# Three buffers of sums instead of four, loaded one place sooner, and three store buffers for the x side and the early sums

## The chip, the cores and the metric

The kernel runs on one core of one Trainium2 chip. The metric is the device time of one execution in microseconds, as the median of the runs. PE is TensorE, PEld its weight loads, DVE is VectorE, ACT ScalarE, POOL GpSimd and SP SyncE; SP issues nearly all DMAs.

## The reference, cut to what matters

Four graph layers on x (64 graphs, 256 nodes, 256 features) with a residual and a layer norm after each. The change touches the first alone, which is a recurrence over the nodes:

```python
d = jnp.sum(adj, axis=-1)
norm_adjT = jnp.swapaxes(adj, 1, 2) * dinv[:, :, None]      # dinv = 1 / d, or 0
def step(h, i):
    x = jnp.take(h_e, i, axis=1)
    row = jnp.take(norm_adjT, i, axis=1)
    x_par = jnp.einsum('bj,bjd->bd', row, h)                # all nodes, the new ones before i
    iou = x @ W_ioux.T + b_ioux + x_par @ W_iouh.T + b_iouh
    r, z = jnp.split(iou, 2, axis=1)
    r, z = (jax.nn.sigmoid(r), jax.nn.sigmoid(z))
    hc = jnp.tanh(x @ W_coux.T + b_coux + x_par * r @ W_couh.T + b_couh)
    h_new = z * x_par + (1.0 - z) * hc
    return jax.lax.dynamic_update_slice(h, h_new[:, None, :], (0, i, 0)), None
h_out, _ = jax.lax.scan(step, h_e, jnp.arange(256))
x = layernorm(x + h_out)
```

## The kernel before, in words

The kernel has three stretches. A head makes, for the first half of the nodes, the part of `x_par` that comes from the old states x (nodes not yet updated), and stores it in a DRAM tensor `Us`. Then 256 steps of the recurrence run, one node each, for all 64 graphs at once. Then the layers 1 to 3 follow graph by graph; the change does not touch them.

**Steps, places, blocks.** Step n stands at place p = n % 8 in block a = n // 8; i = n % 32 is its place in a group of 32 nodes. The loop over the steps has a schedule by hand: each engine runs its instructions in the order in which the program writes them. At the end of each step stand the DMA issues of that step.

**Sums.** `sums[a]`, the tile `ACC` (128 x 8 x 128, 512 KB), holds the unfinished sums of `x_par` for the eight nodes of window a. `sums_in(a)` (line 313) allocates it and loads the x part from `Us` (L316). To it are added: the products with states just made, on DVE (`push`, L645) and on ACT and POOL (`scale_far`, L687, L692, L696; they reach as far as the next window); the `early` part, on POOL at places 3 and 4 (L853), made with states long before and kept in DRAM tensors `Es`; and the `late` part, on POOL at places 6 and 7 (L913). `ready` (L840) is the last reader of a row of `ACC`.

**Early part.** At place 0, `early_in_part(n + 16)` (L453) loads the early part of window a + 2; it is added to `sums[a + 2]` at places 3 and 4 of the same block. Windows from 8 on (node 64) have one, from 24 on (node 192) two.

**Late part.** At places 0 to 3 PE multiplies the states in the ring `Hw` with the adjacency (L531); `send` writes the result to DRAM (`Lb`, L511), `receive` loads it as `late_sb` (L517), and L913 adds it to the next window.

**Fills.** At places 4 to 7 PE has spare work in each step (`fill_early`): the early products (`early`, L424, from states `Hs` and adjacency `A`), or else the x side for the second half of the nodes (`x_side`, `xp`, L213). Their results go from PSUM into a tile `ub` (128 x 4 x 256) by copies on ACT (L256; in the trace `xu` and `eu`), and one step after the second copy, two DMAs store the tile to `Us` (L220) or `Es` (L436). Before, the pool gives `ub` two buffers, so the first copy into a new `ub` waits until the store of the tile two before has landed. The copies stand in a list (`copy_later`, `next_of`) and are taken at fixed points of a step; on ACT the copy at the end of a step stands ahead of the next step's copy `xpT` (L629), for which PE waits with its next matmuls (L620).

**Flush.** At i = 8 and i = 16 (both place 0) `flush` (L655) writes 15 or 16 states per half from the ring to DRAM, two DMAs of packets of 32 KB. The issues of a step's end stand on SP's list in this order: stores that fell due, the early part (place 0), the sums (place 1), xq (place 2), state and flush, the loads of the queue `loads` (state tiles `Hs`, adjacency `A`, `xA`, `xX`; L269).

Before, the sums have four buffers: windows 0, 1 and 2 are loaded ahead of the steps, window 3 in step 1, and at place 1 of block a window a + 3, into the buffer of window a - 1:

```python
            if p == 0 and n + 2 * U < N:
                early_in_part(n + 2 * U)
            if p == 1 and n + 3 * U < N:
                sums_in(n // U + 3)
```

Of the kernel before, what the change touches and what calls it, by code (L numbers as in the profile page):

```python
# [9 lines left out]
F32 = mybir.dt.float32  # L10
# [9 lines left out]
P = 128  # L20
# [50 lines left out]
def _recurrence(tc, ident, Hd, x, adj, W_ioux, b_ioux, W_iouh, b_iouh, W_coux, b_coux, W_couh, b_couh, wide, then):  # L71
# [20 lines left out]
    B, N, D = x.shape  # L92
    T = 32
    NB = N // T
    U = 8
# [8 lines left out]
    with ExitStack() as ctx:  # L104
# [21 lines left out]
        blk = ctx.enter_context(tc.tile_pool(name="r_blk", bufs=2))  # L126
# [83 lines left out]
        def x_product(pb, at, A, Xs):  # L210

            for jc, (a, xs) in enumerate(zip(A, Xs)):
                nc.tensor.matmul(  # L213
                    pb[:, at, :], a, xs, start=(jc == 0), stop=(jc == len(A) - 1)
                )

        def x_out(half, b, ub):

            for c in range(2):
                nc.sync.dma_start(  # L220
                    Us[c, b:b + 4, half * P:(half + 1) * P, :].rearrange("b i f -> i b f"),
                    ub[:, :, c * P:(c + 1) * P],
                )
# [30 lines left out]
        def copy_later(out, in_, then=None):  # L254
            def f(n):
                nc.scalar.copy(out, in_)  # L256
                held.pop(0)
                if then:
                    then(n)

            copies.append(f)

        def load_later(out, in_, rank):

            begun = []

            def f(n):
                with nc.allow_non_contiguous_dma(reason="bias vector across partitions"):
                    nc.sync.dma_start(out, in_)  # L269
                begun.append(n)  # L270

            loads.append((rank, f))
            loads.sort(key=lambda e: e[0])
            return begun

        def landed(begun, n):

            return all(f and n > f[0] + 2 for f in begun)

        def at_step(n, f):  # L280
            transfers.setdefault(n, []).append(f)
# [3 lines left out]
        def base_bank(shape, name):  # L285

            while len(held) == 3:
                next_of(copies, now)
            held.append(name)
            return ps.tile(shape, F32, tag="base", name=name, bufs=3)  # L290
# [21 lines left out]

        def sums_in(a):

            sums[a] = ACC = blk.tile([P, U, P], F32, tag="ACC", name=f"ACC_{a}", bufs=4)
            nc.sync.dma_start(  # L316
                ACC, Us[:, :, a * U:(a + 1) * U, :].rearrange("c b i f -> (c b) i f")
            )
# [3 lines left out]
        def x_side():  # L322

            def load(g):
                A = stream.tile([P, XB, P], F32, tag="xA", name=f"xA2_{g}", bufs=3)
                Xs = stream.tile([P, XB, D], F32, tag="xX", name=f"xX2_{g}", bufs=3)
                return A, Xs, [
                    load_later(to, of.rearrange("b j d -> j b d"), 2)
                    for to, of in ((A, adj[g:g + XB, P:N, P:N]), (Xs, x[g:g + XB, P:N, :]))
                ]  # L330

            def cut(A):
                nc.gpsimd.tensor_mul(A, A, tri.unsqueeze(1).to_broadcast([P, XB, P]))

            tiles = [load(e * XB) for e in range(3)]
            ahead = False
            n = yield
            for g in range(0, B, XB):
                A, Xs, last = tiles.pop(0)
                while not ahead:  # L340
                    if landed(last, n):
                        cut(A)
                        ahead = True
                    n = yield
                ahead = False
                ub = stream.tile([P, 4, D], F32, tag="ub", name=f"xu2_{g}")
                for b in range(0, XB, 2):
                    pb = base_bank([P, 2, D], f"xp2_{g}_{b}")
                    for q in range(2):
                        x_product(pb, q, [A[:, b + q, :]], [Xs[:, b + q, :]])  # L350
                        if q:
                            copy_later(ub[:, b:b + 2, :], pb, None if b + 2 < XB else (
                                lambda n, b=g, ub=ub: at_step(n + 1, lambda: x_out(1, b, ub))
                            ))
                            if b + 2 == XB and g + 3 * XB < B:
                                tiles.append(load(g + 3 * XB))
                        if not ahead and tiles and landed(tiles[0][2], n):

                            cut(tiles[0][0])
                            ahead = True  # L360
                        n = yield
# [13 lines left out]
        early_ub = []  # L375
# [36 lines left out]
        def early_fill(n):  # L412

            if early_pb:
                pb, e = early_pb.pop(), 1
            else:
                if not early_in or not landed(early_in[0][0], n):
                    return False
                _, k, lo, _, t = early_in[0][0:5]
                pb, e = base_bank([P, 2, D], f"early_{k}_{lo}_{t}"), 0  # L420
                early_pb.append(pb)
            _, k, lo, hi, t, Hs, A = early_in[0]
            for q in range(4):
                nc.tensor.matmul(  # L424
                    pb[q * T:(q + 1) * T, e, :], A[0:hi - lo, t % 2 * GB + e * 4 + q, :],
                    Hs[0:hi - lo, e * 4 + q, :], start=True, stop=True,
                )
            if e:
                early_in.pop(0)
                if t % 2 == 0:  # L430
                    early_ub[:] = [stream.tile([P, 4, D], F32, tag="ub", name=f"eu_{k}_{lo}_{t}")]
                ub = early_ub[0]

                def store():
                    for c in range(2):
                        nc.sync.dma_start(  # L436
                            Es[k, lo][c, 2 * t - 2:2 * t + 2].rearrange("n q i f -> (q i) n f"),
                            ub[:, :, c * P:(c + 1) * P],
                        )

                copy_later(
                    ub[:, t % 2 * 2:t % 2 * 2 + 2, :], pb,
                    (lambda n: at_step(n + 1, store)) if t % 2 else None,
                )
            return True

        def early_in_part(first):

            k, i = divmod(first, T)
            for (kk, lo), E in Es.items():  # L450
                if kk == k:
                    part = blk.tile([P, U, P], F32, tag="early", name=f"early_sb_{first}_{lo}")
                    nc.sync.dma_start(  # L453
                        part, E[:, :, :, i:i + U, :].rearrange("c n q i f -> (c n q) i f")
                    )
                    early_parts.append((first, part))
# [106 lines left out]
        def chain_S(k):  # L563

            Sd = blk.tile([P, T], F32, tag="Sd", name=f"Sd_{k}")
            flat = tables[k]["S"].rearrange("p j i -> p (j i)")
            first = (LAG - 1) * T
            nc.vector.tensor_mul(
                Sd, flat[:, first:first + (T - 1) * (T + 1) + 1:T + 1],
                dinv[:, k * T:(k + 1) * T],  # L570
            )
            return Sd
# [128 lines left out]
        sums = {}  # L701
# [9 lines left out]
        with tc.tile_pool(name="r_first_ps", bufs=4, space=bass.MemoryType.PSUM) as xps:  # L711
            for g in range(0, B, GB):
# [4 lines left out]
                for n in range(0, GB, 4):  # L717
                    ub = fst.tile([P, 4, D], F32, tag="ub", name=f"xu_{g}_{n}")
# [25 lines left out]
        stream = ctx.enter_context(tc.tile_pool(name="r_stream", bufs=2))  # L744
        work = ctx.enter_context(tc.tile_pool(name="r_work", bufs=2))
        ps = ctx.enter_context(tc.tile_pool(name="r_ps", bufs=1, space=bass.MemoryType.PSUM))

        sums_in(0)
        warm = work.tile([P, P], F32, tag="ready", name="warm", bufs=1)[:, 0:1]
        nc.vector.memset(warm, 0.0)  # L750
        nc.scalar.activation(warm, warm, AF.Sigmoid)
        tables[0]["An"] = late_load(0)
        tables[0]["Sd"] = chain_S(0)
        for a in range(1, 3):
            sums_in(a)
        for e in range(2):
            flip_x(0, e, xq[0])
            next_of(copies, 0)
# [26 lines left out]
        def fill_early(n):  # L785
            nonlocal x_left
            if not early_fill(n):
                for _ in range(2 if p in (6, 7) else 1):
                    if x_left and not fill(x_left, n):
                        x_left = None  # L790

        ctx.enter_context(tc.manual_schedule())
        for now in range(N):
            n = now
            k, i = divmod(n, T)
            p = n % U
# [119 lines left out]
            for f in transfers.pop(n, ()):  # L916
                f()
            if p == 0 and n + 2 * U < N:
                early_in_part(n + 2 * U)
            if p == 1 and n + 3 * U < N:  # L920
                sums_in(n // U + 3)
            if p == 2 and n // U + 2 < N // U:
                xq[n // U + 2] = load_x(n // U + 2)
            if i == U:
# [584 lines left out]
def kernel(ctx: ExitStack, tc: tile.TileContext, ins, out):  # L1509
# [14 lines left out]
    def load_layers(load):  # L1524
        weights.extend(
            _load_layers(nc, wide, load, ins["L1_gnn_W"], ins["L1_gnn_b"], l2, l3)
        )

    _recurrence(
        tc, ident, Hd, x, adj,  # L1530
        *(ins["L0_gnn_" + n] for n in (
# [44 lines left out]
```

## Time and profile before

| | |
|---|---|
| median of 3 runs | 3242.15 us (3241.41 to 3253.62) |
| profiled execution | 3241.76 us, span 3239.9 us |
| mean granted TensorE clock | 0.978 |
| PE busy in the span | 3038.5 us (94%) |
| DVE, ACT, POOL busy | 2611.5, 1949.4, 1882.3 us |
| head, steps, layers | 0 to 133, 133 to 1425, 1425 to 3240 us |

The span is that of the instructions on the core; the execution's time is 1.9 us longer. A step begins here where the copy `xpT` (L629) starts on ACT, so that step lengths are distances between such copies: 5.04 us in the mean, by place (medians) 6.08, 4.95, 4.69, 4.69, 4.63, 4.64, 4.64, 4.64. Landing times of loads are read from the DMA packets in the trace.

### The profile page before, as it was taken

The page shows a single profiled execution, that of the slowest core. Times are in us where ns is not written, and L with a number is a line of the kernel's source. Part 1 is how long each engine was busy: PE and PEld are TensorE (multiplying, and loading weights), DVE is VectorE, ACT ScalarE, POOL GpSimd, SP SyncE. Part 2 cuts the span into 40 slices and gives each one's busy share as a digit, 9 for nine tenths or more (in the row PEclk, how much of TensorE's full clock was granted, in tenths as well). Part 3 has the DMA queues.
Part 4 walks back from the last instruction along what each step waited for, and adds up shares of the span by engine and source line. Part 5 has one row for each costly group of instructions (what it writes and reads, how often), then busy time and mean ns, then how long its engine had stood idle before and what let it go on. Part 6 is the DMA issues. An engine that isn't in the chain of part 4 may idle for free.

```text
span 3239.9 us, 80388 instructions
## 1 busy us (share of the span) xinstructions
PE 3038.5 (94%) x28076; PEld 2257.2 (70%) x28076; DVE 2611.5 (81%) x7425; ACT 1949.4 (60%) x5160; POOL 1882.3 (58%) x2226
## 2 busy tenths in 40 slices
PE   4799999999999998958999999999999999999997
PEld 3566665655566665636888888888888888888885
DVE  2477776877678878745999999999999999999986
ACT  0166666666566666634666666666666666666664
POOL 2276777776677788733555555555555555555543
PEclk8899999999999999988999999999999999999998
DMA  9866777777776764434344444444444444444421
GB/s 304 255 165 144 195 175 177 175 174 190 182 185 151 193 159 133 100 71 92 81 89 88 88 87 88 88 89 88 88 88 88 88 89 89 89 89 89 89 50 30
DMA packets 954189, 402.54 MB, mean 124 GB/s; under 512 B 664524, under 2 KB 929880, under 8 KB 950104
## 3 DMA queue, kind: packets, MB, share of 16 engines
q1 hardware_dynamic: 935768, 379.42, 50.2%
q10 hardware_dynamic: 18016, 17.96, 1.8%
q8 instruction: 224, 3.67, 0.5%
q14 instruction: 181, 1.48, 0.2%
HBM read 278.53 MB, written 99.61 MB: 117 GB/s over the span
## 4 chain that ended last, share of the span: by engine, by line
PE 83%; DVE 6%; DMA 5%; issue 2%; SPq 1%; POOL 1%; ACT 1%; ACTq 0%; DVEq 0%; POOLq 0%
PE mm L1048 14%; PE rc L620 8%; PE rc L612 5%; PE late L531 4%; PE s L1279 4%; PE mm_2f L1048 4%; PE mm_3v L1048 4%; PE mm_2v L1048 3%; PE mm_t L1048 3%; PE mm_g L1048 3%; PE mm_3f L1048 3%; PE mm_2s L1048 3%; PE mm_2w L1048 3%; PE o L1314 3%; PE z_ps L620 3%; PE z_ps L612 3%
## 5 line engine op out<-in xcount | busy, mean ns | idle before, releaser
L1291 POOL TENSOR_TENSOR p3s<-p 128x256 f32<-128x256 f32 x512 | 358.9, 732 | 259.5 <-ACT p L1289 253.5
L1048 PE MATMUL mm<-xT,weights 128*128 128x256 f32 x2048 | 482.8, 384 | 2.0 <-ACT xT L1163 2.0
L696 POOL TENSOR_TENSOR ACC<-ACC,far 128x640 f32<-128x640 f32 (+2 forms) x312 | 412.9, 1323 | 79.1 <-ACT far L687 42.4
L645 DVE SCALAR_TENSOR_TENSOR ACC<-keep,S,ACC 128x128 f32<-128x128 f32 x1561 | 436.8, 343 | 18.0 <-POOL ACC L913 13.0
L1048 PEld LDWEIGHTS mm<-xT,weights 128*128 128x128 f32 x2048 | 385.9, 191 | 78.6 <-ACT xT L1163 27.8
L1004 ACT ACTIVATE y<-y,shift,rstd 128x256 f32<-128x256 f32 x512 | 279.7, 596 | 161.8 <-DVE shift L1002 161.8
L1288 DVE TENSOR_TENSOR p<-s,neg 128x512 f32<-128x512 f32 x512 | 317.6, 682 | 44.2 <-PE s L1279 44.0
L1289 ACT ACTIVATE p<-p 128x512 f32<-128x512 f32 x512 | 307.2, 629 | 6.8 <-DVE p L1288 6.0
L612 PE MATMUL rc<-WxT,xqT 128*64 128x256 f32 x2048 | 271.6, 386 | 3.3 <-ACT xqT L256 2.2
L996 POOL TENSOR_TENSOR rstd<-rstd,mhalf 128x2 f32<-128x2 f32 x256 | 173.6, 695 | 153.4 <-DVE rstd L995 151.7
L840 POOL TENSOR_TENSOR ready<-ACC,dinv 128x128 f32<-128x128 f32 x255 | 101.9, 400 | 251.8 <-DVE ACC L645 248.8
L692 POOL TENSOR_TENSOR far<-hs,S 128x384 f32<-128x384 f32 (+1 forms) x310 | 222.0, 716 | 4.7
L1328 DVE RECIPROCAL rT<-o 128x256 f32<-128x256 f32 x128 | 223.8, 1748 | 0.0
L992 DVE BATCH_NORM_STATS2 st<-y 128x6 f32<-128x256 f32 x512 | 209.7, 410 | 13.5 <-POOL y L1184 10.7
L1195 ACT ACTIVATE qk<-mm,weights 128x256 f32<-128x256 f32 x256 | 107.2, 470 | 162.4 <-PE mm L1048 157.2
L620 PE MATMUL rc<-WhT,rT 128*64 128x128 f32 x2048 | 171.2, 289 | 34.1 <-DVE rT L863 32.4
L863 DVE TENSOR_TENSOR rT<-rT_ps,xpT 128x128 f32<-128x128 f32 x256 | 74.2, 290 | 151.6 <-PE rT_ps L861 148.5
L620 PE MATMUL rc<-WhT,xpT 128*64 128x128 f32 x2048 | 169.7, 287 | 26.8 <-ACT xpT L629 26.8
L1184 POOL TENSOR_TENSOR y<-y,g 128x512 f32<-128x512 f32 x64 | 81.1, 1268 | 195.3 <-ACT g L1181 195.3
L620 PEld LDWEIGHTS rc<-WhT,rT 128*64 128x64 f32 x2048 | 108.6, 138 | 122.1 <-DVE rT L863 115.4
L620 PEld LDWEIGHTS rc<-WhT,xpT 128*64 128x64 f32 x2048 | 107.6, 137 | 113.4 <-ACT xpT L629 104.8
L531 PE MATMUL late<-Hw,An 64*32 64x256 f32 x3840 | 171.6, 389 | 14.6 <-issue 6.0
(171 smaller groups left out, 7356.5 us busy)
## 6 DMA issues: line engine op xcount, KB each, us to landing
xX<-in_x_dram ACTq DMA_DIRECT2D x16, 1024.0 KB
Us<-xu SPq DMA_DIRECT2D x64, 256.0 KB
ACC<-Us SPq DMA_DIRECT2D x32, 512.0 KB
Es<-eu SPq DMA_DIRECT2D x64, 256.0 KB
early_sb<-Es SPq DMA_DIRECT2D x32, 512.0 KB
xin<-in_x_dram SPq DMA_DIRECT2D x64, 256.0 KB
ad<-in_adj_dram SPq DMA_DIRECT2D x64, 256.0 KB
y<-Hd SPq DMA_DIRECT2D x64, 256.0 KB
```

The costliest lines, as they stand in the source:

```text
L531: nc.tensor.matmul(pb[g][q * T:(q + 1) * T, e, :], An[rows, b].rearrange("p u s -> p (u s)"), Hw[rows, b, :], start=True, stop=True,)
L612: nc.tensor.matmul(G[o * B:(o + 1) * B], xqT[a, i // 2][:, i % 2, kc, h * B:(h + 1) * B], WxT[:, kc, o, gates], start=False, stop=False, s ...
L620: nc.tensor.matmul(G[o * B:(o + 1) * B], hT[:, kc * B:(kc + 1) * B], WhT[:, kc, o, g], start=False, stop=(kc == 1), skip_group_check=True,)
L645: nc.vector.scalar_tensor_tensor(acc[:, 0, :], keep[:, j % 2, :], s, acc[:, 0, :], ALU.mult, ALU.add)
L692: nc.gpsimd.tensor_mul(tmp[:, begun:count, :], hs.unsqueeze(1).to_broadcast(shape), s[:, begun:count].unsqueeze(2).to_broadcast(shape),)
L696: nc.gpsimd.tensor_add(acc, acc, tmp[:, 0:count, :])
L1004: nc.scalar.activation(y[:, c, :], y[:, c, :], AF.Identity, bias=shift[:, c:c + 1], scale=rstd[:, c:c + 1],)
L1048: nc.tensor.matmul(pm[:, c, :], lhsT[:, k, c * P:(c + 1) * P], rhs[:, k, :], start=(k == 0), stop=(k == 1),)
L1288: nc.vector.tensor_add(p, s_ps[i], self.neg3)
L1289: nc.scalar.activation(p, p, AF.Exp, scale=ISQ)
L1291: nc.gpsimd.tensor_add(both, p[:, 0, :], p[:, 1, :])
L1328: nc.vector.reciprocal(rT, o_ps[:, 1, :])
```

## The change

`ACC` gets three buffers instead of four, and window a + 2 is loaded at place 0 of block a, ahead of its early part, into the buffer of window a - 1. Ahead of the steps only windows 0 and 1 are loaded. The tile `ub` of the x side and of the early sums gets three buffers instead of two. A buffer of `ACC` and one of `ub` both take 4 KB of each partition, so the tiles behind them keep their room; the scratch column `warm`, with which ACT loads its Sigmoid table in the head, no longer waits for DMAs of the head (`bias3`, `nat_ih`) and moves up on ACT's list.

```diff
         def sums_in(a):
-            sums[a] = ACC = blk.tile([P, U, P], F32, tag="ACC", name=f"ACC_{a}", bufs=4)
+            sums[a] = ACC = blk.tile([P, U, P], F32, tag="ACC", name=f"ACC_{a}", bufs=3)
...
-                ub = stream.tile([P, 4, D], F32, tag="ub", name=f"xu2_{g}")
+                ub = stream.tile([P, 4, D], F32, tag="ub", name=f"xu2_{g}", bufs=3)
...
-                    early_ub[:] = [stream.tile([P, 4, D], F32, tag="ub", name=f"eu_{k}_{lo}_{t}")]
+                    early_ub[:] = [stream.tile([P, 4, D], F32, tag="ub", name=f"eu_{k}_{lo}_{t}", bufs=3)]
...
-        for a in range(1, 3):
-            sums_in(a)
+        sums_in(1)
...
             if p == 0 and n + 2 * U < N:
+                sums_in(n // U + 2)
                 early_in_part(n + 2 * U)
-            if p == 1 and n + 3 * U < N:
-                sums_in(n // U + 3)
```

## The prediction, made before the changed kernel ran

> **What bounds the kernel now.** I read the stages first: the busy time by stretch, for the head (0 to 133 us), the recurrence (133 to 1425) and the layers behind it. Columns: stretch, length, then busy time and count of PE, PEld, DVE, ACT and POOL, granted clock, DMA share, GB/s.
>
> ```profile
> 133.00:1425.00 1292.00, 1207.98 (x15987) 780.30 (x15986) 974.85 (x3453) 812.33 (x2721) 922.73 (x1053) 0.98 0.67 162
> 1425.00:3240.00 1815.00, 1754.94 (x11784) 1416.83 (x11783) 1599.07 (x3910) 1134.00 (x2433) 931.51 (x1152) 0.98 0.39 85
> ```
>
> PE works 93% of the recurrence, so the change can win only from the 84 us in which PE stands there, and from half-clock stretches; every microsecond won moves the layers, which no edit touches, forward. Next, the waits of that stretch (waiter, what it waited for: total us, times, longest):
>
> ```profile
> POOL ACC L913 <- DMA late_sb<-Lb: 16.3, 7, 5.6
> ...
> ACT xu L256 <- DMA Us<-xu: 6.5, 2, 3.9
> ...
> ACT xu L256 <- DMA Es<-eu: 3.1, 2, 2.2
> ```
>
> The lower two are what a third `ub` buffer is for: ACT's copy into `ub` waits until an older `ub` is stored. For `ACC<-Us` only the start at 133 us waits, and nothing ever for `early_sb`. The chain of waits (start, us, what) has stores on the path:
>
> ```profile
> 211.79 4.55 DMA Us<-xu
> ...
> 375.84 4.55 DMA Us<-xu
> ...
> 500.55 4.52 DMA Es<-eu
> ```
>
> The timeline of PE shows what one wait costs (start, us, what, idle time before it). The last row is the same matmul group in an undisturbed step:
>
> ```profile
> 217.22 0.66 PE L620 MATMUL rc<-WhT,xpT 128*64 128x128 f32 x8 [2.31 <-ACT xpT L629]
> ...
> 219.37 1.12 PE L620 MATMUL rc<-WhT,rT 128*64 128x128 f32 x8
> 220.28 1.88 PE L612 MATMUL rc<-WxT,xqT 128*64 128x256 f32 x8
> ...
> 256.17 1.03 PE L612 MATMUL rc<-WxT,xqT 128*64 128x256 f32 x8
> ```
>
> First PE stands for 2.31 us, then it runs slowly. The granted clock says why: 0.50 in the stretch from 218.6 to 222.0 and in that from 382.4 to 385.8, 1.00 between them.
>
> **The store buffers.** The `ub` copies fall on places 4 to 7 of a block, at most three tiles in a block. With two buffers the third tile waits for the store of the first, issued one to two steps earlier and landing 4.5 us after issue; with three it waits for a tile of the block before, over 20 us old. So I take all these waits as gone: what comes next on ACT, `xpT` L629, has its PE operand long since. PE idled behind them 2.31 us (step 15), 3.57 (47) and 1.86 (71), 7.7 in sum; the fourth wait, 0.9 us at step 39, makes its step 0.2 longer than an equal one (5.42 against 5.23 for steps 23 and 55; a step is the distance between two L629 copies). Behind steps 15 and 47 the half clock makes steps 16 and 48 7.77 us long, where the median of place 0 is 6.08: 1.7 each, 3.4 together. Sum 7.7 + 3.4 = 11.1; ends 7.7 (half clocks come anyway) and 11.9 (against the shortest place 0, 5.69).
>
> The clock needs weighing, because PE ran at half speed after a pause of 2.31 us. The Trainium skill ("TensorE: Matmul & The Clock Gate", Part 1) says that the clock halves after at least one idle window of about 3.4 us; by it only the 3.57 us pause would count, and this term would be 9.4. The 2.31 us row differs from the page, and the measurement decides.
>
> **The moved load, on SP's queue.** The list of the changed kernel's instructions shows the same DMAs. In each block of eight steps the 512 KB load of sums now stands at place 0 behind the stores of `ub`, ahead of the early part and, in 14 blocks, of the flush (L655); before, it stood at place 1 behind all of them and behind the loads of place 0. Its buffer's last reader is `ready` of two steps before, so that wait is met. Queued behind it: the early part (POOL waits, L853, place 3), the flush, then state and A loads (PE, places 4 to 7). It brings 128 packets of 4 KB; the packets of the 32 loads span 1.5 to 6.0 us each, median near 3. I take 2.5 us, as for the early loads beside it.
>
> - L853. The early part of window 200 is issued so on SP (both halves), and used so on POOL:
>
> ```profile
> 1078.48 0.94 SPq L453 DMA_DIRECT2D early_sb<-Es  x2
> ```
>
> ```profile
> 1096.57 2.63 POOL L853 TENSOR_TENSOR ACC<-ACC,early_sb 128x512 f32<-128x512 f32 x2
> ```
>
> Its last packet ends at 1084.2. Over all 24 windows the least margin from last packet to L853 is 9.7 us. Load and early part together need 2.5 more: cost nothing (as far as 6.0 it is still nothing).
> - The flush. In the block of step 136 the queue now reads:
>
> ```profile
> 839.02 0.66 SPq L453 DMA_DIRECT2D early_sb<-Es  x1
> 839.72 0.92 SPq L655 DMA_DIRECT2D Hd<-Hw  x2
> 840.74 4.33 SPq L269 DMA_DIRECT2D Hs<-Hd  x1
> 845.17 4.46 SPq L269 DMA_DIRECT2D A<-in_adj_dram  x1
> 849.72 3.97 SPq L316 DMA_DIRECT2D ACC<-Us  x1
> ```
>
> Behind the flush each issue drags 4 us, while its 32 KB packets (3.8 us each) drain. The load now goes ahead: flush, `Hs` and A land 2.5 us later, what stood behind the load (xq, `Lb`, `late_sb`) carries the same bytes ahead of it and comes no later, up to 4 us sooner by SP's issue time. Late by this is the A of step 140: packets end near 857, first matmul near 859, so 2.5 us later it misses by about 1. I take +1; ends below (the second and third cases).
> - Instruction supply: at 520.97 PE waited 3.93 us for nothing shown, two steps after a flush, while a 16 KB instruction packet came at 518.5. A flush 2.5 us later can shift this by -4 to +3; I take 0.
>
> **Head.** The table load for Sigmoid (1.28 us at 94.65) moves on ACT's list to where ACT waits from 20 to 33 us: hidden before by the wait for PE up to 100.9, hidden after; without cover it would cost 1.3. A few issues wait for another earlier DMA now; the nearest rows, `Us` stores of 1.5 to 2.1 us, bound it at -2 to +2; I take 0, since DMA is busy 99% there either way. The third load of sums still follows the second at once; the fourth moves from step 1 to step 8 and is first read at step 17. The last moves from step 225 to 232, with no stall near.
>
> **Sum.** The profiled execution took 3241.76 us, span 3239.9, 0.4 under the median 3242.15. 3241.8 - 11.1 + 1 = 3231.7; on the median's scale 3232.
>
> **The rivals.**
> *Late parts come later (slower).* If the moved load pushes everything behind the flush, `Lb` and `late_sb` too, by 2.5 us, POOL's L913 at places 6 and 7 waits longer, then DVE and PE. The margins from the last packet of `late_sb` to L913 are thin: in 12 of the 14 flush blocks under 2.5 us, four at 0.4 to 0.5, that is, at the landing itself. With 0.4 us from last packet to use, the shortfalls add to 21 us: 3241.8 - 11.1 + 21 = 3252; with a half clock (1.7) in four of them 3259. It decides from the point where `late_sb` lands more than 1 us later. For it: the thin margins. Against it: bytes ahead of `late_sb` are the same. The Trainium skill ("DMA: Bandwidth & Descriptors", Queues, rings and completion order) says that each DMA engine consumes descriptors in ring order, which speaks for delay of the early part and flush; it leaves `late_sb` where it was. The rows agree as far as issues behind the flush drag.
> *Late parts come sooner (faster).* SP is 4 us sooner at `Lb`, and the stalls behind it in steps 119 (11.34 us against 4.64) and 143 (10.06) go: 12.1 more, 3219. For it: L316's own 3.97 us in the queue; against it: the engines are nearly full there, so transfers set the time.
> *No change.* The `ub` wait was cover: PE's next operand is late by as much, and the 11 us return as other waits: 3242. Against it: `Hw` stores, which the next late matmuls need, were issued 8 us ahead of them at step 16.
>
> **Chances and range.** Forecast 0.60 (3224 to 3242: term ends, instruction supply, head), slower late parts 0.15, sooner 0.15, no change 0.10. A measurement tells 0.5%, 16.2 us, from no change: under 3226 or over 3258. Faster: 0.13 of the sooner case and 0.04 of the forecast's lower end, 0.17. Slower: two thirds of its case and 0.02 of mishaps, 0.12. Same: 0.71. The range of 8 in 10 reaches to both outer cases, 3218 to 3254.
>
> **What would show it.** Right: no wait of `xu` or `eu` for `Us` or `Es`; steps 15, 47, 71 near 5.2 us, 16 and 48 near 6; no half clock there; recurrence 10 us shorter; no POOL wait for `early_sb` or `ACC<-Us`. Wrong: L913's 16.3 us grown or gone, PE `early` waiting for A or `Hs` at place 4, a longer head.

## The result, and the profile after

The changed kernel took 3235.59 us in the median of 9 runs (3228.72 to 3239.96), the kernel before 3244.02 beside it: a ratio of 0.9968 (0.9954 to 0.9982). In a second set it was 3231.72 against 3244.32, 0.9952 (0.9937 to 0.9967). The forecast of 3232 was near in the total, but two of its terms were far off and cancelled. All that follows is about that.

The profiled execution took 3233.59 us (span 3231.6). From the first `xpT` copy to the last, the recurrence went from 1284.3 to 1270.4 us (-13.9); the head ahead of the first copy grew by 2.1, the layers behind the last, which no edit touches, by 3.6. Busy time of the recurrence, after, columns as before:

```profile
135.00:1412.00 1277.00, 1199.88 (x15983) 776.09 (x15984) 976.59 (x3453) 816.47 (x2721) 922.95 (x1053) 0.99 0.66 164
```

PE now stands for 77 us of the recurrence instead of 84. The waits after (waiter, what it waited for: total us, times, longest):

```profile
POOL ACC L912 <- DMA late_sb<-Lb: 9.4, 7, 3.9
...
PE early L424 <- DMA A<-in_adj_dram: 6.0, 2, 4.8
...
PE rc L612 <- issue: 3.7, 1, 3.7
```

No `xu` or `eu` copy waits for a store any more. The wait for `late_sb` (L912, the former L913) fell from 16.3 to 9.4 us. The second row is new; the third stood at 1.1 us before. PE behind the `xpT` copy of step 15, where it had stood for 2.31 us and then run at half clock:

```profile
215.79 0.66 PE L620 MATMUL rc<-WhT,xpT 128*64 128x128 f32 x8
...
218.08 1.03 PE L612 MATMUL rc<-WxT,xqT 128*64 128x256 f32 x8
```

There is no idle time, and the L612 group takes 1.03 us instead of 1.88. Steps 15, 47 and 71 are now 5.23, 5.23 and 4.82 us long, steps 16 and 48 6.17: as forecast. But step 53, 4.66 us before, now takes 12.61. PE in its timeline:

```profile
405.90 0.92 PE L424 MATMUL early<-Hs,A 48*32 48x256 f32 x8 [4.83 <-DMA A<-in_adj_dram]
...
410.98 1.92 PE L612 MATMUL rc<-WxT,xqT 128*64 128x256 f32 x8
```

and the granted clock behind that pause, in the busy times by stretch (first number after POOL's count):

```profile
406.00:409.40 3.40, 3.40 (x29) 2.01 (x32) 0.23 (x2) 0.90 (x4) 0.26 (x1) 0.52 0.71 191
```

This is the pause and half clock of the store waits again, at another place. The reason is on SP's queue: before,

```profile
396.74 0.35 SPq L269 DMA_DIRECT2D A<-in_adj_dram  x1
```

and after,

```profile
395.76 0.35 SPq L269 DMA_DIRECT2D A<-in_adj_dram  x1
```

The first matmul that reads that A came 10.6 us behind the issue before (407.32, no wait) and 10.1 us behind it after (405.90). The compute arrives 6.3 us sooner (step 53 starts at 401.11 instead of 407.43); the load is issued only 1.0 us sooner, and its last completion came at 406.3 us before and 405.8 after (the states of the same product, `Hs`, landed 0.3 us ahead of that). In both traces SP's issues stand back to back, with gaps of 0.2 us at most, from 364 to 394 us, and the two flush issues of step 48 end 0.5 us later than before. That points to SP's list, not the compute, as what set the time of the load.

The sums of step lengths at the places that matter (us; for the variants, see the experiments):

| kernel | store waits: 15, 16, 39, 47, 48, 71 | A: 53 to 55 | late part: 112, 119, 143, 199 | supply: 74, 106, 107 |
|---|---|---|---|---|
| before | 44.2 | 14.5 | 35.6 | 22.1 |
| after | 32.4 | 22.5 | 24.1 | 20.6 |
| after, second profile | 32.4 | 26.2 | 23.8 | 18.4 |
| load ahead, two `ub` | 43.9 | 14.5 | 24.1 | 14.3 |
| load behind, three `ub` | 32.4 | 23.7 | 27.5 | 16.1 |
| load behind, two `ub` | 45.9 | 14.7 | 29.7 | 15.7 |

Before to after: -11.8, +7.9, -11.5 and -1.5; the small differences of the other steps add up to +3. The late part of window 120 shows where the third column comes from. POOL before and after:

```profile
749.99 1.26 POOL L913 TENSOR_TENSOR ACC<-ACC,late_sb 128x512 f32<-128x512 f32 x1 [5.61 <-DMA late_sb<-Lb]
```

```profile
741.00 1.26 POOL L912 TENSOR_TENSOR ACC<-ACC,late_sb 128x512 f32<-128x512 f32 x1 [3.91 <-DMA late_sb<-Lb]
```

Its last packet lands 39.6 us behind the block's start before, 36.3 after; that of window 144 goes from 40.3 to 38.4. The bytes queued ahead of it are the same. One thing that differs is the DMA share (second number from the end; the last is GB/s; a packet is counted whole where it starts, so the share can pass 1) in the stretches of the block from step 112, which starts at 709.87 before:

```profile
709.87:713.87 4.00, 4.00 (x49) 2.96 (x47) 3.23 (x13) 3.31 (x11) 3.59 (x5) 1.00 0.39 118
713.87:737.87 24.00, 22.45 (x340) 13.55 (x338) 18.82 (x67) 15.58 (x51) 17.62 (x21) 1.00 0.99 210
737.87:741.87 4.00, 4.00 (x54) 2.50 (x55) 3.38 (x13) 2.48 (x9) 2.77 (x4) 1.00 1.10 292
```

and at 704.18 after:

```profile
704.18:708.18 4.00, 4.00 (x49) 2.97 (x47) 3.22 (x13) 3.33 (x11) 2.90 (x4) 1.00 0.88 238
708.18:732.18 24.00, 23.99 (x362) 14.49 (x362) 20.01 (x71) 16.70 (x55) 19.07 (x22) 1.00 0.98 228
732.18:736.18 4.00, 4.00 (x54) 2.36 (x52) 3.70 (x14) 2.57 (x10) 2.56 (x5) 1.00 0.74 173
```

In this block the DMA engines were 0.39 busy in the first 4 us and full for the next 28. The moved load begins in the first 4 us (0.88), and at the far end the queue is through sooner (0.74 instead of 1.10). The block of step 136 began with 0.24 before, but not every block begins so: over all blocks place 0 was the fullest place before, 0.96, and place 7 stood at 0.37.

The other thing that differs is SP's list. The stores to `Lb`, which `late_sb` then reads, before and after:

```profile
733.65 4.74 SPq L511 DMA_DIRECT2D Lb<-lb  x2
```

```profile
723.99 4.60 SPq L511 DMA_DIRECT2D Lb<-lb  x2
```

That is 23.8 us behind the block's start before and 19.8 after; `late_sb` is issued at 32.7 and 28.7. In the block of step 136 the issue of `Lb` goes from 27.9 to 25.5. From issue to landing the first `Lb` store at step 112 took 8.2 us before and 8.0 after. So the late parts came sooner by about as much as SP was sooner, and these two traces do not part idle DMA time from SP's list as the reason.

### The profile page after: what moved, and what is told of

The parts are those of the page before. It is cut to its first block, busy times and chain, and to the rows that moved or that the text cites. A ratio compares the mean times of both kernels' runs of the same rounds, so it can differ in the third digit from the quotient of the medians.

```text
span 3231.6 us, 80364 instructions
## 1 busy us (share of the span) xinstructions
PE 3033.7 (94%) x28076; PEld 2255.9 (70%) x28076; DVE 2613.4 (81%) x7425; ACT 1956.6 (61%) x5160; POOL 1882.3 (58%) x2226
## 4 chain that ended last, share of the span: by engine, by line
PE 83%; DVE 6%; DMA 5%; issue 2%; POOL 1%; ACT 1%; SPq 1%; DVEq 0%; ACTq 0%; POOLq 0%
PE mm L1046 14%; PE rc L620 8%; PE rc L612 5%; PE s L1277 4%; PE late L531 4%; PE mm_2f L1046 4%; PE mm_3v L1046 4%; PE mm_2v L1046 3%; PE mm_t L1046 3%; PE mm_g L1046 3%; PE mm_3f L1046 3%; PE mm_2w L1046 3%; PE mm_2s L1046 3%; PE o L1312 3%; PE z_ps L620 3%; PE z_ps L612 3%
## 5 line engine op out<-in xcount | busy, mean ns | idle before, releaser
L1046 PEld LDWEIGHTS mm<-xT,weights 128*128 128x128 f32 x2048 | 387.8, 192 | 79.5 <-ACT xT L1161 27.9
L612 PE MATMUL rc<-WxT,xqT 128*64 128x256 f32 x2048 | 267.6, 381 | 5.9 <-issue 3.7
L990 DVE BATCH_NORM_STATS2 st<-y 128x6 f32<-128x256 f32 x512 | 209.7, 410 | 14.7 <-POOL y L1182 11.8
L687 ACT ACTIVATE far<-hs,S 128x128 f32<-128x128 f32 x534 | 185.1, 401 | 0.8 <-POOL ACC L696 0.5
L531 PE MATMUL late<-Hw,An 64*32 64x256 f32 x3840 | 169.8, 388 | 14.4 <-issue 5.8
```

The costliest lines, as they stand in the source:

```text
L531: nc.tensor.matmul(pb[g][q * T:(q + 1) * T, e, :], An[rows, b].rearrange("p u s -> p (u s)"), Hw[rows, b, :], start=True, stop=True,)
L612: nc.tensor.matmul(G[o * B:(o + 1) * B], xqT[a, i // 2][:, i % 2, kc, h * B:(h + 1) * B], WxT[:, kc, o, gates], start=False, stop=False, s ...
L1046: nc.tensor.matmul(pm[:, c, :], lhsT[:, k, c * P:(c + 1) * P], rhs[:, k, :], start=(k == 0), stop=(k == 1),)
```

## The experiments

Theory A, formed from these two traces: the load's new place carries the gain, and the third store buffer nets little, because PE then meets the A load sooner. The rival: the store buffer carries the gain, as forecast. Why the place counts is settled only in part: the second set (the load behind with two buffers, the changed kernel again, small flush packets with two buffers and on the kernel before) asked whether it was the drag of about 4 us on each issue behind the flush's 32 KB packets, the third (four buffers of sums, and both helpers) whether it was the unused DMA time shown above. The expectations of the first set name their own theories. Times are medians, ratios are to the kernel before on the same chip, whose medians in the three sets are 3246.81, 3244.32 and 3243.56. Executions of one kernel spread by up to 24 us, so sizes are taken from ratios and places from profiles.

### The two edits apart

Load ahead, two store buffers (the changed kernel without the third `ub` buffer):

```diff
-  ub = stream.tile([P, 4, D], F32, tag="ub", name=f"xu2_{g}", bufs=3)       # and eu
+  ub = stream.tile([P, 4, D], F32, tag="ub", name=f"xu2_{g}")
```

> The changed kernel with two ub buffers again: only the sums are changed (three buffers, load at place 0). Theory A (the third ub buffer brings the gain, the moved load about nothing): no gain over before, ratio 0.998 to 1.002; the waits of xu and eu for the stores Us and Es are back at 8 to 10 us in sum, with half clocks behind steps 15 and 47; no wait of early for its loads at step 53. Theory B (the moved load brings a good part of it, since nothing of 512 KB stands behind the flush any more and late_sb comes sooner): ratio 0.996 to 0.998, L913's wait for late_sb near 9 us as in the changed kernel, against 16.3 before.

Measured: 3233.45 us, 0.9949 (0.9932 to 0.9966). The waits for the stores are back:

```profile
ACT xu L256 <- DMA Us<-xu: 6.1, 2, 3.6
ACT xu L256 <- DMA Es<-eu: 3.3, 2, 2.1
```

so are the long steps 15, 47 and 71, and step 53 is 4.65 us. The whole gain is there all the same.

Load behind, three store buffers (three buffers of sums, load still at place 0, but issued behind early part, state and flush):

```diff
             if p == 0 and n + 2 * U < N:
-                sums_in(n // U + 2)
                 early_in_part(n + 2 * U)
...
                 flush(n - T // 2, n - 1)
+            if p == 0 and n + 2 * U < N:
+                sums_in(n // U + 2)
```

> The changed kernel with the load of sums still at place 0, but issued behind the early part, state_out and the flush instead of ahead of them. Theory A: within 3 us of the changed kernel, ratio to before 0.996 to 0.998, the waits for the ub stores gone as there. Theory B: the load behind the flush costs again what it cost before: L913's wait for late_sb back near 16 us, ratio 0.998 to 1.001. Both: no wait for the sums at L853 as long as the load lands within 12 us.

Measured: 3245.32 us, 0.9997 (0.9985 to 1.001). The gain is gone, with the third store buffer in place and steps 15, 47 and 71 short; in the waits:

```profile
POOL ACC L912 <- DMA late_sb<-Lb: 11.3, 7, 5.5
...
PE early L424 <- DMA A<-in_adj_dram: 8.5, 4, 5.5
```

Load behind, two store buffers (both of these edits), and the changed kernel once more:

> Three buffers of sums, the load of sums at place 0 but behind the early part, state and flush, and two store buffers as before. With three store buffers this place of the load gave 0.9997. Theory A: the store buffer nets nothing in either place of the load, so again 0.999 to 1.001 (about 3245 us), steps 119 and 143 as long as before, step 53 back at 4.65 us, steps 15, 47 and 71 long again. Theory B: without the third store buffer 8 to 11 us are lost: 1.0025 to 1.0035, about 3253 us.

> The changed kernel once more, beside the three below. Theory A (the load ahead of the flush carries the whole gain, the third store buffer nets nothing because what it wins at steps 15, 47 and 71 returns at step 53 behind the state and A loads): ratio to the kernel before near 0.996, about 3232 to 3236 us, and within 0.2% of the kernel with the moved load and two store buffers (0.9949). Theory B (the third store buffer is worth its 11 us in most executions, step 53 was one profile's accident): clearly under that kernel's ratio, 0.992.

Measured: 1.001 (0.9999 to 1.0022), 3247.41 us; and 0.9952 (0.9937 to 0.9967), 3231.72 us. So the third store buffer is worth about 0.1% with the load behind (0.9997 against 1.001), and between nothing and a loss of 0.2% with the load ahead (0.9952 and 0.9968 against 0.9949), with intervals that overlap each time. The place of the load is worth 0.3 to 0.6%. The table of steps agrees for the buffers: each of the three profiles with three store buffers has the 11.8 us at the store waits, and each pays 7.9 to 11.6 of it at steps 53 to 55. For the load it shows less than the ratios do, since the two profiles with the load behind are executions 7 and 8 us under their medians.

### Is it the place, or the flush?

First early product with states 0 to 47 allowed one step later (aimed at step 53), on the changed kernel:

```diff
-                if not early_in or not landed(early_in[0][0], n):
+                if not early_in:
+                    return False
+                first = early_in[0][3:5] == (48, 0)
+                if not landed(early_in[0][0], n, 3 if first else 2):
```

> The changed kernel, but the first early product with states 0 to 47 (due in step 53, where PE waited 4.83 us for its loads) may start one step later; x-side products fill its place. Theory A (the time won with the store buffers reached this load, which did not get faster): step 53 falls from 12.6 us to 4.7, and no other step takes the wait over; 8 us less than the changed kernel, ratio to before 0.993 to 0.996. Rival (the DMA queue as a whole is behind by then, so the next product or late_sb waits instead): step 54 or 55 grows by 4 us or more, ratio 0.996 to 0.998 as with the changed kernel.

Measured: 3230.61 us, 0.9952 (0.9938 to 0.9967). Step 53 is short again, but step 55 takes 9.26 us (5.23 before) and step 71 6.91, so that 53 to 55 add up to 18.8. The stall was moved more than removed.

Flush in four DMAs per half, packets of 8 KB, on the changed kernel; with two store buffers; and on the kernel before:

```diff
-                    nc.sync.dma_start(
-                        Hd[lo:end, g * HB:(g + 1) * HB, :], Hw[at:at + end - lo]
-                    )
+                    for b in range(0, HB, HB // 4):
+                        nc.sync.dma_start(
+                            Hd[lo:end, g * HB + b:g * HB + b + HB // 4, :],
+                            Hw[at:at + end - lo, b:b + HB // 4],
+                        )
```

> The changed kernel with the flush cut into four DMAs per half, so packets of 8 KB instead of 32 KB; same bytes, six more issues on SP in a flush block. Theory C (the 32 KB packets hold all queues of the DMA engines, which delays late_sb, the loads of states and the instruction packets): the issues behind the flush fall from 4 us to under 2 us, PE's waits for nothing shown (3.71 us at step 106) fall under 1.5 us, late_sb waits under 5 us; 5 to 12 us less than the changed kernel, ratio to before 0.993 to 0.996. Rival (the bytes count, not the packets): the same waits, and six issues of 0.6 us more push late_sb: ratio 0.997 to 1.000.

> The changed kernel with the flush in four DMAs per half (packets of 8 KB instead of 32 KB) and two store buffers instead of three; with three it gave 0.9925. Theory A: the same within 0.2%, about 3222 to 3229 us; step 53 at 4.65 us instead of 13.2, steps 15, 47 and 71 longer by 8 us in sum with their half clocks. Theory B: the store buffer's 11 us are lost: 0.9955 to 0.996, about 3233 us.

> The kernel before with one edit: the flush in four DMAs per half (packets of 8 KB instead of 32 KB). The load of sums stays at place 1 behind it, four buffers of sums, two store buffers. Theory A in its strong form (what the load stood behind was the drag of the 32 KB packets on the queue, 4 us for each issue behind them): the small packets alone give what the moved load gave or more, 0.992 to 0.995, 3220 to 3228 us, with steps 119 and 143 shorter and the issues behind the flush near 1 us. Rival (the 512 KB of the load themselves, ahead of the late parts, set the time, whatever the packets): ratio 0.999 to 1.001.

Measured: 3223.8 us, 0.9925 (0.9913 to 0.9938), the fastest of all; 3229.82 us, 0.995 (0.9933 to 0.9966); and 3240.38 us, 0.999 (0.9978 to 1.0002). So theory A in its strong form, that the small packets alone give what the moved load gave, fell: with the load left behind them they give nearly nothing, and steps 119 and 143 stay long (10.14 and 8.45). The run does not clear SP's list, though. A flush is now eight issues instead of two, and in the block of step 112 SP reaches the load of sums at 13.1 us (10.4 before) and `Lb` at 24.6 (23.8): SP was not made any sooner. On top of the moved load and two store buffers they give nothing either (0.995 against 0.9949). Only with both edits do they gain some 0.3 to 0.4%; step 53 is as long as in the changed kernel (13.23), and I found no single place for it. (Against the profile of the changed kernel, steps 74, 106 and 107 are 6.2 us shorter and the late part's steps 2.4 longer.)

The place alone, with four buffers of sums and two store buffers as in the kernel before: place 0 ahead of the flush, place 7, place 3.

```diff
-            if p == 1 and n + 3 * U < N:
+            if p == 7 and n + 3 * U < N:       # or 3; for place 0 the call stands ahead of early_in_part
                 sums_in(n // U + 3)
```

> The kernel before (four buffers of sums, two store buffers) with the load of window a + 3 at place 0, ahead of the early part and the flush, instead of place 1. Theory A (the load goes into DMA time that is unused at the start of a block, so the late parts land 1 to 3 us sooner): the gain of the kernel with three buffers and the same place, 0.9949, returns: 0.993 to 0.997, about 3224 to 3235 us. Rival (it was the later window or the changed head, not the place): 0.999 to 1.001.

> The kernel before with the load of window a + 3 at place 7 instead of place 1. There the DMA engines are busy 0.34 of the time, at places 0 to 4 0.73 to 1.08. Theory A (unused DMA time): 0.992 to 0.996, 3218 to 3231 us, L913's waits for the late part under 9 us in sum. Rival (only the order against the flush counts): the same as place 0 ahead of the flush, 0.995. Second rival (the place is worth nothing): 0.999 to 1.001.

> The kernel before with the load of window a + 3 at place 3 instead of place 1: still behind the flush, state and A loads, and just ahead of the late parts, in DMA time that is full. Theory A: late_sb lands up to 3 us later in the flush blocks, L913's waits grow over 25 us, 1.001 to 1.005, 3247 to 3260 us. Rival (the drag of the issues right behind the flush set the time; at place 3 it is over): 0.995 to 0.998.

Measured: place 0, 3234.86 us, 0.9972 (0.9959 to 0.9985); place 7, 3234.85 us, 0.9974 (0.9961 to 0.9987); place 3, 3259.59 us, 1.0046 (1.0028 to 1.0064). The waits for the late part are 7.5 us in sum at place 7, and at place 3:

```profile
POOL ACC L913 <- DMA late_sb<-Lb: 24.3, 14, 5.4
```

Place 3 shows that distance from the flush is not enough: there the load is far from it, and the kernel is slower. In the block of step 112 SP issues `Lb`, no longer behind the load, at 22.0 us (23.8 before), but the load now stands between `Lb` and `late_sb`, which is issued at 32.3 (32.7 before). Place 3 costs in two ways. The late parts of ordinary blocks land later (window 176 at 33.5 us behind the block's start, 30.3 before; window 208 at 35.0, 30.5 before, but there it is nearly as late with the load at place 7), though those of windows 120 and 144 do not (39.3 and 40.0), which the expectation had wrong. And the `ub` stores are slower too: ACT's waits for `Us` and `Es` grow from 9.6 to 14.4 us in sum. Places 0 and 7 gain the same, about 9 us, as the rival "only the order against the flush counts" had it, though the DMA share before was so different at the two (0.96 and 0.37 over all blocks). The larger gain that theory A allowed for place 7 did not come in the median, although its profiled execution (span 3219.2), the fastest of its 12, has the shortest recurrence of all, 1263.8 us. Shown, then, is that the load costs time behind the flush and costs more just ahead of the late parts. Whether the first of these is a matter of SP's list, of the flush's packets or of idle DMA time, these runs do not part. The gain of places 0 and 7 is a little under that of the three-buffer kernel (0.9949), with intervals that overlap.

Both helpers on the changed kernel:

> The changed kernel with both edits that were tried alone: the first early product with the states 0 to 47 may begin one step later (alone 0.9952), and the flush in four DMAs per half (alone 0.9925). If their gains lie at different places (step 53, and the flush blocks from step 104 on): 0.989 to 0.992, 3209 to 3218 us. If what the first wins at step 53 comes back at steps 55 and 71 as it did alone: 0.992 to 0.994, 3218 to 3225 us.

Measured: 3232.24 us, 0.9966 (0.9951 to 0.998). Neither sum came: it is slower than with the small packets alone. Step 119 is back at 10.07 us, 143 at 9.02 and step 21 at 9.81, behind A loads and late parts. Each kernel in this family shifts the time at which loads meet their readers, and a few microseconds more or less of lead make or lose such stalls.

## Why the prediction was right and wrong

- **The store buffers at their own places: right.** Forecast 11.1 us, measured 11.8 (44.2 to 32.4), no wait for a store, no half clock at steps 15, 16, 47 and 48.
- **"I take all these waits as gone", with nothing late next: wrong.** The step that failed is the search for what is late next. It looked at `xpT`'s PE operand and, for the third rival, at the `Hw` stores, not at the loads of states and A, of which the first is read at step 53. In the trace of before that A was used 10.6 us behind its issue without a wait; its landing moved by 0.5 us, the compute by 6.3. This is the mechanism of the rival "no change", with 7.9 us of the 11.8 at steps 53 to 55 (11.6 in the second profile). The load ahead with two buffers loses nothing by having the waits back.
- **The moved load: wrong, and this is the largest error.** Forecast +1 us. The ratios of pairs with the load ahead and behind give 0.3 to 0.6%, 9 to 20 us of gain. The step that failed is the price of nothing for "up to 4 us sooner by SP's issue time", with the reason, in the second rival, that "the engines are nearly full there, so transfers set the time". SP did issue `Lb` 4.0 us sooner in the block of step 112 and 2.4 in that of step 136, as that rival said, and from issue to landing the first store of step 112 took no longer than before. Nor were the engines nearly full throughout: the DMA share at the start of these two blocks was 0.39 and 0.24, which the whole-recurrence share of 0.67 had hidden. The rival "late parts come sooner" was the mechanism: step 143 fell from 10.06 to 4.64 us as it said, step 119 from 11.34 to 9.34 only. Whether SP's issue time or the idle DMA time carried it is not shown.
- **The +1 itself** (A of step 140): no wait of `early` for A at that step; the two that there are stand at steps 21 (1.18 us) and 53. L853 (L852 after) never waits for `early_sb`, as forecast.
- **Slower late parts:** did not come; L912's waits fell to 9.4 us. That rival's mechanism exists, as the load at place 3 shows (24.3 us, 1.0046), but with the load just ahead of the late parts.
- **Instruction supply:** taken as 0. The stall of 3.93 us at step 74 went (-6.4 us in the step), and one came at step 106 (+3.6, with +1.3 in step 107):

```profile
677.34 0.58 PE L612 MATMUL rc<-WxT,xqT 128*64 128x256 f32 x1 [3.71 <-issue]
```

  In sum -1.5, inside the bounds of -4 to +3.
- **The clock:** the 4.83 us pause at step 53 ended in half speed, the 1.18 us pause at step 21 did not. The Trainium skill ("TensorE: Matmul & The Clock Gate", Part 1) has the clock halve after at least one idle window of about 3.4 us; these two rows agree with it. The prediction took the 2.31 us pause for the one that differs, but it is not alone: the granted clock fell to 0.50 also where PE's longest pause just before was 1.41 us (ending at 446.4 us in the kernel before), 2.01 (at 841.3 there) or 2.11 (at 831.3 in the changed kernel), and it stayed at 1.00 after one of 1.86 (at 506.4 before). The length of a single pause does not decide it in these traces.
- **Head and layers:** the head's +2.1 is half taken back by steps 0 to 7 (1.1 shorter). The layers' 3.6 us are no effect of the edits: over the 14 profiles of this study that stretch took 1820.8 to 1827.4 us with the same code.

The sum of the forecast's terms, -10.1, and the 8.2 us between the two profiled executions thus agree by two errors: some 7 us too much for the buffers, some 12 too little for the load (about 4 and 11.5 measured in these profiles, against 11.1 and -1). That the total came out near was luck. The other small terms, head and layers among them, make up the rest.

What stays open: whether the load's place acts by SP's list, by the flush's packets or by idle DMA time, why small flush packets gain only with both edits together, and why the place-7 load is not better in the median than place 0.

## What to carry to other kernels

Before a reordering of equal bytes is called neutral, read the DMA share in stretches of a few microseconds, and the issue times on SP, around both places: here a load moved from behind the flush to ahead of it let what is queued behind both be issued and land sooner, and the same load just ahead of the late parts cost time. When a wait is removed, list every load that is read in the next steps with its margin, since loads that keep their absolute time take the gain back. A sum that comes out right should still be checked term by term with the edits apart.

## What the runs showed of the hardware that was not expected

- The stall for instructions at the place-2 step two steps behind a flush (step 74 or 106) made that step 8.5 to 11.1 us long in five of the ten profiles with 32 KB flush packets (before, after twice, place 0, place 3), and in none of the four with 8 KB packets (4.7 to 4.9 us). Counting every pause of PE over 1 us put down to "issue" at these two steps, it is eight of the ten and none of the four. In each of the five a 16 KB instruction packet landed inside the stall. That the flush's packets hold it up is a reading of these profiles, not a test.
- One 512 KB load of the same bytes is worth from -0.3% to +0.5% by its place within the block of eight steps alone (places 0 and 7 against place 3, the rest of the kernel equal).
